# The last graph layer's weight products as seven block products, a block product accumulated in PSUM, and a plan with measured durations

## The chip, the cores and the metric

The kernel runs on one core of one Trainium2 chip. The metric is the device time of one execution in microseconds; the kernel before took 1390.6 us, the median of three executions between 1390.11 and 1391.59 us. The engines are named as in the profile: PE is TensorE (PEld its weight loads), DVE is VectorE, ACT is ScalarE, POOL is GpSimd, and SP is the queue that issues most transfers.

## The reference

Four graph layers act on 64 graphs of 256 nodes with 128 features, all in fp32, and each ends in a layer norm of the input plus the layer's output. Cut to what matters here:

```python
# layer 0: attention over pairs; layer 1: masked attention (both cut)
# layer 2: a gated update, five times
def step(h, _):
    m_in = jnp.einsum('nm,bmd->bnd', in_matrix, h)      # both matrices are adj
    m_out = jnp.einsum('nm,bmd->bnd', out_matrix, h)
    av = jnp.concatenate([m_in, m_out], axis=-1)
    u3 = h @ u3_w.T + u3_b
    z = sigmoid(av @ w3_w.T + w3_b + u3)
    r = sigmoid(av @ w4_w.T + w4_b + u3)
    hv = tanh(av @ w5_w.T + w5_b + (r * h @ u5_w.T + u5_b))
    return (1.0 - z) * h + z * hv, None
# layer 3: x, A x, A^2 x, A^3 x for two equal adjacencies, each with its weights
parts = [x[..., None], chebyshev(adj0, x, 3), chebyshev(adj1, x, 3)]
y = jnp.einsum('bnik,iok->bno', jnp.concatenate(parts, axis=3), weight_1)
x = layernorm(x + y)
```

Since both adjacencies are the same matrix A, layer 3 is x W0' + A x W1 + A^2 (x W2 + A x W3): W0' is the first weight plus the identity (the residual), and W1 to W3 are each the sum of two weights. The kernel takes it in this form.

## The kernel before

The 64 graphs are worked in 32 units of two. Ten units are in flight, one in each lane; a planner in the kernel's Python sorts all instructions by a greedy simulation with a duration and a latency for each, and then records them in that order. The planner's numbers decide the order on each engine, and nothing else.

A product of A (256 by 256, two by two blocks of 128) with a unit's features (two graphs, each two blocks of 128 columns) is done with seven block products in place of eight, with sums of blocks ahead (`block_sums`) and merges afterwards. `left_fast` does this 182 times, in layer 2 and at the start of layer 3:

```python
def left_fast(src, blk, mat, s, p1, m, by_pool):
    four = block_sums(src, blk, s, by_pool)        # three GpSimd instructions
    x, y = bank(), bank()                          # two PSUM banks
    ...
    one(x, 0, a(0), 0, 0, (src,))                  # one(): a product 128x128x128
    add(ACT, 280, lambda: nc.scalar.copy(p1.ap[:, 0:P], x.ap[:, 0:P]), (x,), (p1,))
    one(x, 1, a(1), 1, 0, (src,))
    one(y, 3, a(3), 3, 1, (src,), s.writers[-1:])
    one(y, 1, sm(0), 3, 0, (s,))
    one(y, 0, sm(1), 2, 0, (s,))
    one(x, 2, sm(2), 2, 1, (s,))
    one(y, 2, sm(3), 1, 1, (s,))
    merged(x, y, p1, m)                            # L872, L875, L877, L878

def merged(x, y, p1, m):
    # L872: m[0], m[3] = x[1:3] + p1                128x256 VectorE
    # L875: m[1:3] = y[0:2] + m[3]                  128x256
    # L877: m[3] = y[0] + m[2]                      128x128
    # L878: m[1:3] = y[2:4] + m[1:3]                128x256
```

In layer 3, `xT` and `aT` (x and A x, features on the partitions) are multiplied by the weights with eight products of 256 columns, whose results are a pair: the part for A^2 and the part that is added directly. The part for A^2 is copied by ScalarE, summed by VectorE and multiplied by A^2 (`a2f`) with seven block products that run into the same banks:

```python
for k, src in enumerate((xT, aT)):
    for (b, c), (ps, at) in home.items():          # four places in two banks
        add(PE, mm_ns(N), ... nc.tensor.matmul(
            gd(ps.ap)[:, at], bn(src.ap)[:, b, c * P : (c + 1) * P], w3.ap[:, k], ...))   # L1004
...
add(ACT, 370, lambda: nc.scalar.copy(sv[:, 0:4:3], gd(x.ap)[:, 0:3:2]), ...)              # L1009
add(ACT, 370, lambda: nc.scalar.copy(sv[:, 1:3], gd(y.ap)[:, 0:2]), ...)                  # L1010
block_sums(s, lambda g: sv[:, g], L["xT1"], -1 in BY_POOL)                                # on VectorE
... seven products (L1015), a ScalarE copy of the first (L1028)
merged(x, y, p1, out)
add(DVE, 240, ... out[3] += x[3] ...)                                                     # L1035
layernorm(u, L, y_pairs(out))
```

The last three units (`PLAIN = 3`) take another form, `layer3_end`: eight weight products and four products with A^2, all of 256 columns (L1048, L1055).

Of the kernel before, what the change touches and what calls it, by code (L numbers as in the profile page):

```python
# [32 lines left out]
PERIOD = 43e3  # L33
TAIL = 0.3
LATE = 6
PACE = 3.0
PACE_GATED = 1.56
# [4 lines left out]
HASTE = {"pe": 10e3, "act": 10e3, "dve": 10e3}  # L42
PLAIN = 3
# [26 lines left out]
class Plan:  # L70
# [5 lines left out]
    LATENCY = {"pe": 500, "dve": 400, "act": 400, "pool": 500, "sp": 4000}  # L76
# [127 lines left out]
def kernel(  # L204
# [58 lines left out]
    def lane_cells(k):  # L263
# [8 lines left out]
        for at, halves in (("e", (("r", "ex"), ("z",))), ("p", (("v",), ("xT1",)))):  # L272
            for half, names in enumerate(halves):
                over = [c[at]]
                for name in names:
                    c[name] = Cell(c[at].ap.rearrange("p g n -> p (g n)")[:, half * T : (half + 1) * T], over=over)
                    over = [*over, c[name]]
        c["x"] = cell(f"x_{k}", [P, UB, NC, D])
# [112 lines left out]
    add(ACT, 500, lambda: nc.scalar.copy(adjT.ap.rearrange("p c n -> p (c n)"), ps_adj.ap), (ps_adj,), (adjT,))  # L391
# [81 lines left out]
    add(ACT, 500, lambda: nc.scalar.copy(adjTp.ap.rearrange("p c n -> p (c n)"), ps_adjp.ap), (ps_adjp,), (adjTp,))  # L473
# [18 lines left out]
    w3 = cell("w3", [D, 2, 2, D])  # L492
    add(POOL, 480, lambda: nc.gpsimd.tensor_add(w3.ap[:, 0, 1, :], wk.ap[:, :, 0], ident.ap), (wk, ident), (w3,))
    for k in range(1, 4):
        add(POOL, 480, lambda k=k: nc.gpsimd.tensor_add(
            w3.ap[:, k % 2, 1 - k // 2, :], wk.ap[:, :, k], wk.ap[:, :, k + 3]), (wk,), (w3,))
# [10 lines left out]
    fast_blocks(a2f, a2T)  # L507
    plan.rank = None


    X = {}

# [17 lines left out]
    def feature_major(src, view, t):  # L530
        ps = bank()
        for g in range(G):
            add(PE, 110, lambda g=g: nc.tensor.transpose(ps.ap[:, g * P : (g + 1) * P], view(g), ident.ap),
                (src, ident), (ps,))
        add(ACT, 500, lambda: nc.scalar.copy(t.ap, ps.ap), (ps,), (t,))

    def turned(u, L, step):
# [8 lines left out]
        add(DVE, 1050, lambda: nc.vector.transpose(  # L546
# [33 lines left out]
    def layernorm(u, L, pairs, swap=False, centred=False):  # L580
# [11 lines left out]
        add(POOL, 1050, lambda: nc.gpsimd.tensor_tensor(rstd.ap, ve.ap, nhalf.ap, op=ALU.pow), (ve, nhalf), (rstd,))  # L592
        by_act = u >= TIGHT and plan.layer in NORM

        if by_act and not centred:
            mean = st.ap.rearrange("p k (j s) -> p k j s", j=2)[:, :, :, 1]
            if "shift" in SMALL:
                add(POOL, 280, lambda: nc.gpsimd.tensor_scalar_mul(
# [50 lines left out]
    def layer0(u, L):  # L649
# [47 lines left out]
        for b in range(UB):  # L697
            add(DVE, 520, lambda b=b: nc.vector.tensor_add(
                ev[:, b, :, 0:P].rearrange("p k (c i) -> p k c i", c=NC), rv()[:, b].rearrange("p c (i k) -> p k c i", k=2),
                neg0.ap[:, :, 0:P].rearrange("p k (c i) -> p k c i", c=NC)), (row, neg0), (e,), group=es)  # L700
# [8 lines left out]
        for b in range(UB):  # L709

            small(u, "s", 130, lambda eng, b=b: eng.tensor_scalar(
# [3 lines left out]
        for g in range(G):  # L715
            add(ACT, 400, lambda g=g: nc.scalar.activation(
# [4 lines left out]
        for g in range(G if SCALES and u >= TIGHT else 0):  # L721
            add(ACT, 320, lambda g=g: nc.scalar.activation(
# [33 lines left out]
    def layer1(u, L):  # L756
# [6 lines left out]
        for bs in [[b] for b in range(UB)] if u < HALVES else [list(range(UB))]:  # L763
# [3 lines left out]
            for b in bs:  # L767
                for g in range(b * NC, (b + 1) * NC):
                    add(ACT, 600, lambda g=g, b=b: nc.scalar.activation(  # L769
# [15 lines left out]
            for b in bs:  # L785
# [11 lines left out]
                for c in range(NC if SCALES and u >= TIGHT else 0):  # L797
                    add(ACT, 290, lambda b=b, c=c, ov=ov: nc.scalar.activation(
# [11 lines left out]
        add(ACT, 550, lambda: nc.scalar.activation(ex.ap, hp.ap, AF.Exp, bias=minus1.ap), (hp, minus1), (ex,))  # L810
        xf = X[u].ap.rearrange("p b c d -> p (b c d)")
        add(DVE, 600, lambda: nc.vector.scalar_tensor_tensor(hp.ap, ex.ap, 1.0, hp.ap, op0=ALU.min, op1=ALU.max), (ex, hp), (hp,))
        add(DVE, 600, lambda: nc.vector.tensor_add(hp.ap, hp.ap, xf), (hp, X[u]), (hp,))
# [11 lines left out]
    def block_sums(src, blk, s, by_pool):  # L825
# [5 lines left out]
        wide, narrow = (830, 480) if by_pool else (360, 220)  # L831
# [7 lines left out]
    def left_fast(src, blk, mat, s, p1, m, by_pool):  # L839
# [3 lines left out]
        def one(ps, at, lhs, k, c, cells, after=()):  # L843
            add(PE, mm_ns(P) + 4, lambda: nc.tensor.matmul(  # L844
                ps.ap[:, at * P : (at + 1) * P], lhs(), mat.ap[:, k, c * P : (c + 1) * P], start=True, stop=True,
                skip_group_check=True), (*cells, mat), (ps,), after, group=four)
# [8 lines left out]
        one(x, 0, a(0), 0, 0, (src,))  # L855
        add(ACT, 280, lambda: nc.scalar.copy(p1.ap[:, 0:P], x.ap[:, 0:P]), (x,), (p1,))  # L856
        one(x, 1, a(1), 1, 0, (src,))
        one(y, 3, a(3), 3, 1, (src,), s.writers[-1:])
# [4 lines left out]
        merged(x, y, p1, m)  # L863

    def merged(x, y, p1, m):
        mv = gd(m.ap)

        def pv(ps):
# [3 lines left out]
        add(DVE, 400, lambda: nc.vector.tensor_tensor(  # L872
            mv[:, 0:4:3], pv(x)[:, 1:3], p1.ap[:, 0:P].rearrange("p (o n) -> p o n", o=1).to_broadcast([P, 2, P]), op=ALU.add),
            (x, p1), (m,))
        add(DVE, 400, lambda: nc.vector.tensor_tensor(  # L875
            mv[:, 1:3], pv(y)[:, 0:2], mv[:, 3:4].to_broadcast([P, 2, P]), op=ALU.add), (y, m), (m,))
        add(DVE, 240, lambda: nc.vector.tensor_add(mv[:, 3:4], pv(y)[:, 0:1], mv[:, 2:3]), (y, m), (m,))  # L877
        add(DVE, 400, lambda: nc.vector.tensor_add(mv[:, 1:3], pv(y)[:, 2:4], mv[:, 1:3]), (y, m), (m,))  # L878

    def layer2(u, L):  # L880
        h, ht = turned(u, L, -1), X[u]
        for step in range(STEPS):
# [14 lines left out]
            if not fast:  # L897
                add(ACT, 500, lambda ps_m=ps_m: nc.scalar.copy(m.ap, ps_m.ap), (ps_m,), (m,))
# [15 lines left out]
            add(ACT, 600, lambda ps_g=ps_g, up=up: nc.scalar.activation(  # L914
                r.ap, ps_g.ap, AF.Tanh, bias=bias2.ap[:, 1:2], scale=0.5 / up), (ps_g, bias2), (r,))
            tanh_r = list(r.writers)
            add(DVE, 600, lambda h=h: nc.vector.scalar_tensor_tensor(r.ap, r.ap, 1.0, h.ap, op0=ALU.add, op1=ALU.mult),
# [4 lines left out]
            add(ACT, 600, lambda ps_g=ps_g, up=up: nc.scalar.activation(  # L922
# [6 lines left out]
            add(DVE, 600, lambda h=h, new=new: nc.vector.scalar_tensor_tensor(  # L929
                new.ap, z.ap, -1.0, h.ap, op0=ALU.add, op1=ALU.mult), (z, h), (new,))  # L930
            add(ACT, 600, lambda ps_v=ps_v, up=up: nc.scalar.activation(  # L931
                v.ap, ps_v.ap, AF.Tanh, bias=bias2.ap[:, 2:3], scale=1 / up), (ps_v, bias2), (v,))
            add(DVE, 600, lambda: nc.vector.scalar_tensor_tensor(v.ap, z.ap, 1.0, v.ap, op0=ALU.add, op1=ALU.mult),  # L933
                (v, z), (v,))
            add(DVE, 600, lambda new=new, part=part: nc.vector.scalar_tensor_tensor(
# [3 lines left out]
            if step < STEPS - 1 and far(u, step):  # L939
# [3 lines left out]
                add(DVE, 600, lambda h=h, v=v: nc.vector.transpose(  # L943
# [10 lines left out]
            if far(u, step):  # L954

                add(DVE, 600, lambda h=h, v=v: nc.vector.transpose(
# [13 lines left out]
            if step < STEPS - 1:  # L970
                add(ACT, 500, lambda ps_t=ps_t: nc.scalar.copy(L["ht"].ap, ps_t.ap), (ps_t,), (ht,))
# [11 lines left out]
    def layer3(u, L):  # L983
# [5 lines left out]
        else:  # L989
# [3 lines left out]
            add(ACT, 500, lambda: nc.scalar.copy(aT.ap, ps_a.ap), (ps_a,), (aT,))  # L993
# [6 lines left out]
        x, y = bank(), bank()  # L1000
        home = {(0, 0): (x, slice(0, 2)), (1, 1): (x, slice(2, 4)), (0, 1): (y, slice(0, 3, 2)), (1, 0): (y, slice(1, 4, 2))}
        for k, src in enumerate((xT, aT)):
            for (b, c), (ps, at) in home.items():
                add(PE, mm_ns(N), lambda k=k, src=src, c=c, b=b, ps=ps, at=at: nc.tensor.matmul(  # L1004
                    gd(ps.ap)[:, at], bn(src.ap)[:, b, c * P : (c + 1) * P], w3.ap[:, k],
                    start=(k == 0 and b == 0), stop=(k == 1), skip_group_check=True), (src, w3), (ps,), tail)
        four, sv = gd(L["xT1"].ap), gd(s.ap)
        copies = object()
        add(ACT, 370, lambda: nc.scalar.copy(sv[:, 0:4:3], gd(x.ap)[:, 0:3:2]), (x,), (s,), group=copies)  # L1009
        add(ACT, 370, lambda: nc.scalar.copy(sv[:, 1:3], gd(y.ap)[:, 0:2]), (y,), (s,), group=copies)  # L1010
        block_sums(s, lambda g: sv[:, g], L["xT1"], -1 in BY_POOL)
        t, p1, out = L["xT1"], L["v"], L["ht"]

        def one(ps, at, lhs, c, k, start, after=()):
            return add(PE, mm_ns(P) + 4, lambda: nc.tensor.matmul(  # L1015
                ps.ap[:, at * P : (at + 1) * P], a2f.ap[:, k // NC, k % NC * P : (k % NC + 1) * P], lhs(), start=start,
                stop=True, skip_group_check=True), (c, a2f), (ps,), after, group=four)

        def d(g):
            return lambda: sv[:, g]  # L1020

        def sm(k):
            return lambda: four[:, k]


        done = [one(x, 1, d(1), s, 2, False)]
        one(x, 0, d(0), s, 0, True, done)
        add(ACT, 280, lambda: nc.scalar.copy(p1.ap[:, 0:P], x.ap[:, 0:P]), (x,), (p1,))  # L1028
        done = [one(y, 3, d(3), s, 7, False), one(y, 2, sm(3), t, 3, False)]
        one(y, 1, sm(0), t, 6, True, done)  # L1030
        one(y, 0, sm(1), t, 4, True, done)
        one(x, 2, sm(2), t, 5, True, done)
        merged(x, y, p1, out)
        mv = gd(out.ap)
        add(DVE, 240, lambda: nc.vector.tensor_add(mv[:, 3:4], gd(x.ap)[:, 3:4], mv[:, 3:4]), (x, out), (out,))  # L1035
# [3 lines left out]
    def layer3_end(u, L, xT, aT, s, tail):  # L1039
# [11 lines left out]
        for c in range(NC):  # L1051
            add(ACT, 300, lambda c=c: nc.scalar.copy(s.ap[:, c * N : (c + 1) * N], ps[c].ap[:, 0:N]), (ps[c],), (s,), group=ps)
        for c in range(NC):
            for mc in range(NC):
                add(PE, mm_ns(N), lambda c=c, mc=mc: nc.tensor.matmul(  # L1055
                    ps[c].ap[:, N : 2 * N], a2T.ap[:, mc, c * P : (c + 1) * P], s.ap[:, mc * N : (mc + 1) * N],
                    start=False, stop=(mc == NC - 1), skip_group_check=True), (a2T, s), (ps[c],))
        pairs = [(ps[c], lambda c=c: view(c)[:, 1]) for c in range(NC)]
# [56 lines left out]
```

The softmax here doesn't subtract the row's maximum and nothing guards it: scores larger than these inputs give would overflow.

## Time and profile before

| | before |
|---|---|
| time, median of three | 1390.6 us |
| span of the profiled execution | 1390.3 us |
| mean granted TensorE clock | 1.000 |
| TensorE busy | 1379.5 us |
| VectorE busy | 1217.7 us |
| ScalarE busy | 909.1 us |
| GpSimd busy | 630.5 us |
| DMA moved | 147.12 MB |

A line of instruction groups reads: source line, engine, operation, output and inputs by the program's names, shapes, count; then the group's busy time in us and the mean of one in ns; then the idle time of the engine ahead of them and what ended it. Names of tiles that share memory may stand for one another (`e` holds the tiles `r` and `z`, `p` holds `v` and `xT1`). In a line of waits the three numbers are the sum in us, how often, and the longest. In the chain of work that ended last, a piece has its start, its length and its number of records.

### The profile page before, as it was taken

How to read it: one execution, taken by the hardware profiler on the slowest of the kernel's cores; microseconds unless marked ns; L12 is line 12 of the kernel's file. 1: busy time of each engine (PE TensorE's matmuls, PEld its weight loads, DVE VectorE, ACT ScalarE, POOL GpSimd, SP SyncE). 2: the span in 40 equal slices, each digit the busy share in tenths (PEclk: the TensorE clock that was granted, in tenths of full speed). 3: DMA queues.
4: the chain of work that ended last, by engine and by line, in shares of the span. 5: the costliest groups of instructions: out<-in, count | busy, mean ns of one | idle time of the engine just before them, and what ended most of it. 6: DMA issues, size and time to landing. Idle time of an engine off the chain costs nothing.

```text
span 1390.3 us, 23222 instructions
## 1 busy us (share of the span) xinstructions
PE 1379.5 (99%) x6891; PEld 967.8 (70%) x6891; DVE 1217.7 (88%) x2745; ACT 909.1 (65%) x2121; POOL 630.5 (45%) x1039
## 2 busy tenths in 40 slices
PE   9999999999999999999999999999999999999998
PEld 8776666677667777667767767776666666666777
DVE  6887999999888989989898999899889798988955
ACT  6988554655676676865776768877675556564544
POOL 4233344345354453544453554465444443644524
PEclk9999999999999999999999999999999999999999
DMA  4223454445454545554554544455544545544422
GB/s 119 49 60 95 98 113 98 116 109 121 107 121 106 118 105 114 122 118 112 112 117 105 124 111 113 105 111 125 118 106 98 114 108 104 123 100 107 104 64 61
DMA packets 530076, 147.12 MB, mean 106 GB/s; under 512 B 456480, under 2 KB 495136, under 8 KB 529952
## 3 DMA queue, kind: packets, MB, share of 16 engines
q1 hardware_dynamic: 529152, 145.13, 46.5%
q8 instruction: 55, 0.90, 0.3%
q14 instruction: 69, 0.57, 0.1%
q10 hardware_dynamic: 800, 0.52, 0.1%
HBM read 81.10 MB, written 64.46 MB: 105 GB/s over the span
## 4 chain that ended last, share of the span: by engine, by line
PE 94%; DVE 3%; ACT 1%; POOL 0%; issue 0%; DMA 0%; POOLq 0%; SPq 0%; DVEq 0%; ACTq 0%
PE ps L902 48%; PE ps L844 20%; PE ps L1004 7%; PE ps L780 4%; PE ps L743 4%; PE ps L1015 3%; PE ps L792 2%; PE ps L738 2%; PE ps L667 2%; PE ps L821 1%; PE ps L1048 1%; PE ps L1055 0%; DVE st L587 0%; PE ps L351 0%; PE ps L968 0%
## 5 line engine op out<-in xcount | busy, mean ns | idle before, releaser
L902 PE MATMUL ps<-m,gT 128*128 128x512 f32 x960 | 471.5, 593 | 0.9 <-DVE m L878 0.5
L902 PEld LDWEIGHTS ps<-m,gT 128*128 128x128 f32 x960 | 170.3, 190 | 136.8 <-issue 115.9
L589 POOL TENSOR_SCALAR ve<-st 128x4 f32<-128x4 f32 x110 | 34.9, 317 | 364.9 <-DVE st L587 347.1
L914 ACT ACTIVATE e<-ps,bias 128x512 f32<-128x512 f32 x160 | 109.7, 686 | 130.2 <-PE ps L902 125.8
L931 ACT ACTIVATE p<-ps,bias 128x512 f32<-128x512 f32 x160 | 110.0, 687 | 90.3 <-PE ps L902 87.7
L592 POOL TENSOR_TENSOR rstd<-ve,nhalf 128x4 f32<-128x4 f32 x126 | 145.6, 1156 | 43.8 <-DVE ve L589 33.7
L902 PE MATMUL ps<-e,u5T 128*128 128x512 f32 x320 | 163.4, 593 | 0.0
L922 ACT ACTIVATE e<-ps,bias 128x512 f32<-128x512 f32 x160 | 109.7, 686 | 80.7 <-PE ps L902 78.6
L844 PE MATMUL ps<-adjTp,e 128*128 128x128 f32 x968 | 148.2, 275 | 0.4 <-ACT e L856 0.4
L933 DVE SCALAR_TENSOR_TENSOR p<-e,p 128x512 f32<-128x512 f32 x160 | 117.2, 733 | 33.1 <-ACT p L931 32.1
L844 PEld LDWEIGHTS ps<-adjTp,e 128*128 128x128 f32 x968 | 131.0, 192 | 19.0 <-issue 14.5
L833 POOL TENSOR_TENSOR e<-ht 128x256 f32<-128x256 f32 x121 | 99.4, 821 | 89.0 <-DMA ht<-hb 67.9
L844 PEld LDWEIGHTS ps<-adjTp,ht 128*128 128x128 f32 x726 | 108.7, 191 | 40.8 <-issue 36.7
L844 PE MATMUL ps<-adjTp,ht 128*128 128x128 f32 x726 | 120.8, 275 | 0.0
L902 PEld LDWEIGHTS ps<-e,u5T 128*128 128x128 f32 x320 | 59.2, 190 | 65.9 <-issue 50.1
L611 ACT ACTIVATE x<-ht,ve,rstd 128x128 f32<-128x128 f32 x212 | 90.9, 487 | 13.9 <-POOL ve L600 13.6
L902 PE MATMUL ps<-xT,gT 128*128 128x512 f32 x192 | 98.3, 593 | 0.5 <-DVE m L872 0.5
L833 POOL TENSOR_TENSOR e<-x 128x256 f32<-128x256 f32 x61 | 48.2, 790 | 96.2 <-ACT x L611 83.9
L875 DVE TENSOR_TENSOR m<-ps,m 128x256 f32<-128x256 f32 x182 | 74.8, 413 | 13.4 <-PE ps L844 11.1
L769 ACT ACTIVATE e<-m,esd 128x256 f32<-128x256 f32 x116 | 84.5, 765 | 0.0
L872 DVE TENSOR_TENSOR m<-ps,e 128x256 f32<-128x256 f32 x182 | 74.4, 413 | 11.2 <-PE ps L844 6.9
L835 POOL TENSOR_TENSOR e<-e,ht 128x128 f32<-128x128 f32 x121 | 79.4, 657 | 5.9
(210 smaller groups left out, 3145.7 us busy)
## 6 DMA issues: line engine op xcount, KB each, us to landing
hb<-p SPq DMA_DIRECT2D x182, 256.0 KB, 2.1
ht<-hb SPq DMA_DIRECT2D x484, 64.0 KB, 2.5
xT<-hb SPq DMA_DIRECT2D x244, 64.0 KB, 2.5
m<-row SPq DMA_DIRECT2D x58, 256.0 KB, 3.6
hb<-p SPq DMA_DIRECT2D x124, 64.0 KB, 1.8
ht<-hb SPq DMA_DIRECT2D x31, 256.0 KB, 3.0
out_dram<-x SPq DMA_DIRECT2D x30, 256.0 KB, 2.4
m<-in_x_dram SPq DMA_DIRECT2D x88, 64.0 KB, 2.3
```

The costliest lines, as they stand in the source:

```text
L592: add(POOL, 1050, lambda: nc.gpsimd.tensor_tensor(rstd.ap, ve.ap, nhalf.ap, op=ALU.pow), (ve, nhalf), (rstd,))
L611: add(ACT, 400, lambda j=j, b=b, ch=ch, view=view, at=at, shift=shift, col=col: nc.scalar.activation(X[u].ap[:, b, ch, :], view()[:, j, :] ...
L769: add(ACT, 600, lambda g=g, b=b: nc.scalar.activation(e.ap[:, g, :].rearrange("p (c n) -> p c n", c=NC), ev()[:, b], AF.Prelu, bias=esd.ap ...
L833: add(by, wide, lambda: eng.tensor_sub(four[:, 0:2], blk(slice(2, 3)).to_broadcast([P, 2, D]), blk(slice(0, 4, 3))), (src,), (s,), group=ss)
L835: add(by, narrow, lambda: eng.tensor_sub(four[:, 2:3], four[:, 1:2], blk(slice(0, 1))), (src, s), (s,), group=ss)
L844: add(PE, mm_ns(P) + 4, lambda: nc.tensor.matmul(ps.ap[:, at * P : (at + 1) * P], lhs(), mat.ap[:, k, c * P : (c + 1) * P], start=True, st ...
L902: add(PE, mm_ns(T), lambda: nc.tensor.matmul(ps.ap, w(), rhs.ap, start=start, stop=stop, skip_group_check=True), (c, rhs), (ps,), after)
L914: add(ACT, 600, lambda ps_g=ps_g, up=up: nc.scalar.activation(r.ap, ps_g.ap, AF.Tanh, bias=bias2.ap[:, 1:2], scale=0.5 / up), (ps_g, bias2 ...
L922: add(ACT, 600, lambda ps_g=ps_g, up=up: nc.scalar.activation(z.ap, ps_g.ap, AF.Tanh, bias=bias2.ap[:, 0:1], scale=0.5 / up), (ps_g, bias2 ...
L931: add(ACT, 600, lambda ps_v=ps_v, up=up: nc.scalar.activation(v.ap, ps_v.ap, AF.Tanh, bias=bias2.ap[:, 2:3], scale=1 / up), (ps_v, bias2), ...
L933: add(DVE, 600, lambda: nc.vector.scalar_tensor_tensor(v.ap, z.ap, 1.0, v.ap, op0=ALU.add, op1=ALU.mult), (v, z), (v,))
L1004: add(PE, mm_ns(N), lambda k=k, src=src, c=c, b=b, ps=ps, at=at: nc.tensor.matmul(gd(ps.ap)[:, at], bn(src.ap)[:, b, c * P : (c + 1) * P], ...
```

## The change

It has three parts. First, the weight products of layer 3 use the scheme of seven block products too: the two by two blocks of weights (`w3f`, prepared once with their block sums) against the two "rows" x and A x, where each block product is 128 wide and done for two column blocks of nodes. GpSimd forms four sums of the inputs ahead of them, VectorE merges their results, and the block sums of the closing product with A^2 move from VectorE to GpSimd. 30 units do so (`PLAIN = 2`). Second, in `left_fast` the second block product is accumulated onto the first in PSUM, after ScalarE has copied the first out, instead of being added by VectorE. Third, the planner's durations are replaced by measured ones, and its settings of urgency and latency by others. The first part is meant to take work from TensorE, the second from VectorE, and the third to give an order that fits the chip.

```diff
-LATE = 6
-PACE = 3.0
-PACE_GATED = 1.56
+LATE = 5
+PACE = 3.5
+PACE_GATED = 1.5
-HASTE = {"pe": 10e3, "act": 10e3, "dve": 10e3}
-PLAIN = 3
+HASTE = {"pe": 20000.0, "act": 20000.0, "dve": 20000.0}
+PLAIN = 2
-    LATENCY = {"pe": 500, "dve": 400, "act": 400, "pool": 500, "sp": 4000}
+    LATENCY = {"pe": 600, "dve": 500, "act": 500, "pool": 500, "sp": 4000}
... (durations: ScalarE copies 500 -> 475, VectorE 600 -> 680, and so on)
 # left_fast
-        one(x, 0, a(0), 0, 0, (src,))
-        add(ACT, 280, lambda: nc.scalar.copy(p1.ap[:, 0:P], x.ap[:, 0:P]), (x,), (p1,))
-        one(x, 1, a(1), 1, 0, (src,))
+        one(x, 0, a(0), 0, 0, (src,), start=True)
+        held = [add(ACT, 160, lambda: nc.scalar.copy(p1.ap[:, 0:P], x.ap[:, 0:P]), (x,), (p1,))]
+        one(x, 0, a(1), 1, 0, (src,), held)
+        add(ACT, 160, lambda: nc.scalar.copy(gd(m.ap)[:, 0], x.ap[:, 0:P]), (x,), (m,), group=ms)
...
+        add(DVE, 200, lambda: nc.vector.tensor_add(gd(m.ap)[:, 3], gd(x.ap)[:, 2], p1.ap[:, 0:P]), (x, p1), (m,), group=ms)
-        add(DVE, 400, ... mv[:, 0:4:3], pv(x)[:, 1:3], p1 ...)
 # layer 3
-        ... eight products of 256 columns, two ScalarE copies, block_sums on VectorE
+        x, ya, yb, z = bank(), bank(), bank(), bank()
+        ... four GpSimd sums of 128x256 over x and A x
+        for c in range(NC):
+            one(x, 2 * c, blk(x0, c), (xT,), w3f, 0, start=not c, after=tail)
+        held = [add(ACT, 270, lambda: nc.scalar.copy(gd2(p1.ap), gd2(x.ap)[:, 0:3:2]), (x,), (p1,))]
+        for c in range(NC):
+            one(x, 2 * c, blk(a0, c), (aT,), w3f, 2, after=held)
+        for c in range(NC):
+            one(x, 2 * c + 1, blk(sums[2], c), (sb_,), w3f, 5)
+        ... and eight more: sums[1] by block 4 and sums[0] by block 6 into ya,
+        ... sums[3] by block 3 and a1 by block 7 into yb
+        ... VectorE: up = x[1::2] + p1 (256); mv = ya + up (512); up = ya[:256] + mv[256:] (256); mv = yb + mv (512)
+        ... GpSimd: block sums of the part for A^2 (256, 128, 128 columns)
+        ... seven block products with A^2 into z and x, one ScalarE copy
+        ... VectorE: five merges (256, 256, 128, 256, 256), the last adds the direct part
         layernorm(u, L, y_pairs(out))
```

## The prediction

> **What bounds the kernel now.** I read the page first (busy shares, then the chain that ended last), then TensorE's waits, then the chain in a late stretch, because the pieces there show what one product costs when nothing holds it up.
>
> ```profile
> span 1390.3 us, 23222 instructions
> PE 1379.5 (99%) x6891; PEld 967.8 (70%) x6891; DVE 1217.7 (88%) x2745; ACT 909.1 (65%) x2121; POOL 630.5 (45%) x1039
> ...
> PE 94%; DVE 3%; ACT 1%; POOL 0%; issue 0%; DMA 0%; POOLq 0%; SPq 0%; DVEq 0%; ACTq 0%
> ```
>
> TensorE is busy 99% of the span and the last chain is almost wholly its own. The waits of TensorE say how much of the rest could still be had:
>
> ```profile
> PE ps L351 <- POOL ident masks.py:199: 1.3, 1, 1.3
> PE ps L792 <- DVE m L872: 0.7, 1, 0.7
> PE ps L667 <- ACT xT L535: 0.6, 1, 0.6
> ...
> PE ps L902 <- ACT e L914: 0.2, 1, 0.2
> PE ps L792 <- ACT xT L783: 0.2, 1, 0.2
> ```
>
> There are nine lines, each a single wait, with 4.9 us in total. The busy sum by stretches shows TensorE's last work ending at about 1384.3; the 6.0 us after it are the last normalisation and store. So 1390.3 = 1379.5 + 4.9 + 6.0, within rounding: to shorten the kernel, TensorE must get less work. The prices, from the chain between 1344 and 1365 us (start, length, group, records):
>
> ```profile
> 1347.34 1.73 PE ps L1004 x8
> ...
> 1362.30 0.89 PE ps L1015 x8
> ```
>
> One fp32 product leaves two records in the trace (800 products 512 wide stand in the program, 1600 records in the trace). So a 128x256 product costs 1.73 / 4 = 0.432 us and a 128x128 product 0.89 / 4 = 0.2225 us. Two halves cost 0.445 us, 3% more than one whole.
>
> **What the skill says.** (1) The Trainium skill, "Perfetto Trace Analysis", Identifying the Most-Contended Engine: matmul busy time is a poor measure of nearness to the roofline, since matmuls are pipelined. So I checked it by spacing: summing, over all matmul records, the median distance from start to start for their width gives 1372.8 us, within 7 us of the busy time. Here the 99% is honest. (2) "TensorE: Matmul & The Clock Gate", Back-to-back issue gap: a matmul costs its columns plus a few ns. The trace agrees in form (median record spacing 112, 216 and 429 ns for 128, 256 and 512 columns); that is why splitting a product costs so little. (3) "SBUF — State Buffer", Who interferes with whom: a VectorE instruction with two SBUF inputs contends with a GpSimd instruction that reads SBUF; one with a PSUM input doesn't. The trace agrees: the four 128x512 scalar_tensor_tensor groups of layer 2 average 734 ns, but those with no GpSimd work beside them 680 ns; the adds at L872 average about 413 ns either way, because one input is PSUM.
>
> **The change part by part.**
>
> *Weight products of the last layer.* Before, 29 units of batch pairs do 8 products of 256 columns and 7 of 128 there, and three plain units do 12 of 256. After, 30 units do 14 + 7 products of 128, and two stay plain. The built programs agree: 427 more products 128 wide, 244 fewer 256 wide, everything else on TensorE the same. Per ordinary unit 8 x 0.432 - 14 x 0.2225 = 3.456 - 3.115 = 0.341 us saved, times 29 = 9.9 us. The unit that changes camp: 12 x 0.432 - 21 x 0.2225 = 5.184 - 4.673 = 0.5 us. Sum 10.4 us of TensorE work; with the program's counts and the median spacings above (244 x 0.432 - 427 x 0.224) it is 9.8. I take 10.1.
>
> *VectorE and GpSimd pay for it.* The rows I use:
>
> ```profile
> L872 DVE TENSOR_TENSOR m<-ps,e 128x256 f32<-128x256 f32 x182 | 74.4, 413 | 11.2 <-PE ps L844 6.9 <-ACT e L856 3.6
> L877 DVE TENSOR_TENSOR m<-ps,m 128x128 f32<-128x128 f32 x182 | 49.7, 279 | 0.6
> L833 POOL TENSOR_TENSOR e<-ht 128x256 f32<-128x256 f32 x121 | 99.4, 821 | 89.0 <-DMA ht<-hb 67.9 <-PE ps L902 10.0 <-PE ps L844 5.0
> L1009 ACT COPY e<-ps 128x256 f32<-128x256 f32 x29 | 10.8, 371 | 19.8 <-PE ps L1004 17.2 <-DVE m L878 2.6
> L856 ACT COPY e<-ps 128x128 f32<-128x128 f32 x182 | 47.9, 265 | 44.9 <-PE ps L844 41.5 <-DVE ht L812 1.9 <-DVE st L587 0.4
> ```
>
> In the last layer VectorE gets, per unit, two adds 128x512 (estimate 0.68 us each, from the 134 ns that 128 columns add between the rows of 256 and 128), six of 256 (0.413) and one of 128 (0.279): 4.1 us. It gives up the old merge (1.8 us) and the three block sums, which move to GpSimd (1.1 us). Over 30 and 29 units that is 124 - 84 = +40 us. GpSimd gets four sums of 128x256 (about 0.8 us each) and the three block sums (2.1 us): 5.3 us x 30 = +159 us, a busy share of about 57%. ScalarE loses one 0.37 us copy per unit, -10 us.
>
> *Left products of layers 2 and 3.* 182 of them. The second block product now adds onto the first in PSUM, once ScalarE has copied the first out; a second ScalarE copy takes the sum. VectorE's first merge shrinks from 256 to 128 columns: 182 x 0.134 = -24 us. ScalarE: 182 x 0.265 = +48 us. TensorE does the same products.
>
> *Sums.* VectorE 1218 + 40 - 24 = 1234, plus some 9 us of port contention (640 instructions, 54 ns lost on average now, growing with GpSimd's share from 45 to 57%): 1243, 90%. ScalarE 947, 69%. All stay under TensorE's 1369, and all lie beside it. On the path that sets the end only TensorE's 10.1 us count.
>
> *New waits on TensorE.* The held product: in the new order the TensorE work between the first block product and the one that accumulates on it is 0.67 us at least, over 1.30 in 95% of the 182. The round trip needs about 0.5 (0.2 until the copy starts, 0.265 for it, and the hand-over): it is covered unless ScalarE is over 0.8 us late. For the last layer's four adds and three GpSimd sums before the closing products, the distance is 5.1 us at least and 7.4 in the median; the chain's durations sum to 2 x 0.41 + 2 x 0.68 + 2.1 = 4.3 us. Covered too, with little room in a few units.
>
> *The plan.* Measured durations and new urgency settings only reorder; no work changes. They can touch the 4.9 us of waits, of which about 2 us belong to the first 40 us.
>
> **The rivals.** *A: TensorE work decides* (as above): 1390.6 - 10.1 = 1380.5. For it: one engine at 99%, nine small waits. *B: VectorE and GpSimd become the bound in the full stretches.* VectorE already works 184.65 of the 200 us between 200 and 400 us (92%), and GpSimd's extra reads lengthen its two-input instructions. Against: ten units are in flight, and at 90 to 92% TensorE lost 1.6 us in that stretch and nothing in the next ones. If each of the 30 units cost TensorE one added wait of 0.3 us, 9 us would be gone and the time would be 1389. *C: the new plan also removes the mid-run waits.* Those after 40 us are at most about 3 us: 1377.5. *D: the narrower products cost more than their columns*, since 14 weight loads replace 8 and the load must hide under a shorter product. Against: the 0.2225 us is taken from a run of 128-wide products that already load new weights each time. If each cost another 10 ns, 427 x 0.01 = 4.3 us would be lost: 1385. Four instead of two PSUM banks held in the last layer belong to B: a late bank makes TensorE wait in the same way.
>
> **Range and chances.** A is most likely; B and D pull up by a few us in part, C pulls down by one or two. I take 1380.3, with 1376.5 (A and all of C) to 1386 (half of the gain lost). 2% would be 27.8 us; TensorE's remaining work of 1362 us and the closing 6 us forbid a gain of that size, and a loss of it would need waits of 38 us: faster 0.01, same 0.97, slower 0.02.
>
> **What would show each step.** Right: TensorE's busy time near 1369 with its share still 99%, records +366 in all (2 x 183), GpSimd near 790, VectorE near 1243, ScalarE near 947, TensorE's waits still under 8 us. The held product should appear among TensorE's waits with under 2 us. Wrong: a TensorE share of 98% or less with waits on the last layer's GpSimd sums or adds (B), or 128-wide products spaced wider than 112 ns a record (D).

## The result and the profile after

The changed kernel takes 1398.45 us (median; 1397.92 to 1399.00), the kernel before 1391.09 us in the same comparison: a ratio of 1.0053, 95% interval 1.0036 to 1.0070. It is slower by about 7 us where 10 us less were predicted, outside the predicted range of 1376.5 to 1386.

The page of the changed kernel (span, busy sums, chain by engine), in the lines that answer those shown of before:

```profile
span 1396.1 us, 24423 instructions
PE 1376.1 (99%) x7257; PEld 971.6 (70%) x7257; DVE 1251.7 (90%) x2783; ACT 932.0 (67%) x2274; POOL 816.6 (58%) x1254
...
PE 78%; DVE 12%; POOL 4%; ACT 2%; issue 2%; DMA 1%; SPq 0%; POOLq 0%; DVEq 0%; ACTq 0%
```

TensorE is still "busy 99%", yet the last chain is TensorE's own only to 78% where it was 94%: VectorE and GpSimd now stand in it. TensorE's waits, the largest (sum in us, how often, longest):

```profile
PE ps L852 <- ACT e L864: 2.0, 1, 2.0
...
PE ps L1032 <- DVE e L1061: 1.1, 1, 1.1
PE ps L910 <- DVE m L886: 1.1, 3, 0.5
PE ps L1032 <- ACT e L1042: 0.9, 2, 0.5
...
```

All eleven lines sum to 8.8 us, against 4.9 before. That can't be all, so I made an account by spacing, from the one profiled execution of each kernel. Each matmul record is given the median distance to the next one for its width (112 ns for 128 columns, 216 for 256, 429 for 512); the sum of what the distances have beyond that is the wait. "Tail" runs from the start of the last matmul record to the end. About 1.3 us before the first matmul complete each row. All in us:

| kernel | span | products | waits to 40 us | waits 40 to 1340 us | waits after 1340 us | tail |
|---|---|---|---|---|---|---|
| before | 1390.3 | 1372.8 | 4.9 | 5.1 | 0.2 | 6.0 |
| changed | 1396.1 | 1363.2 | 4.5 | 16.3 | 0.2 | 10.6 |
| difference | +5.8 | -9.6 | -0.4 | +11.2 | 0.0 | +4.6 |

So the gain on TensorE is there (-9.6) and is spent twice: on mid-run waits (+11.2) and on a longer tail (+4.6). The busy share hides this, because a matmul's record (275 ns for 128 columns) reaches over the next ones, so a pause loses up to 160 ns from sight, and a product at half clock counts as busy.

**The tail.** The chain of the changed kernel from its last products on:

```profile
1384.72 1.13 PE ps L1032 x10
1385.85 0.03 issue
...
1385.95 0.44 DVE ht L1083
...
1388.65 0.68 DVE st L595 x2
...
1389.92 1.00 POOL rstd L600
...
1391.23 0.49 ACT x L619
...
1392.11 0.77 ACT x L619 x2
```

And before, after a last piece of TensorE that ends at 1384.33 us:

```profile
1384.42 0.44 DVE st L629
...
1385.14 0.70 POOL rstd L632
...
1387.14 0.46 ACT x L636
```

The unit that `PLAIN = 2` moved into the block form now ends last: five VectorE merges, shared with the neighbour's work, then the statistics of the whole unit, GpSimd's power, four ScalarE instructions and a store of 256 KB. Before, the last unit in the plain form needed no merge, normalised each half apart and stored by halves of 128 KB.

**The largest mid-run wait.** The pause at 373 us, followed back by the chain (start, length, what):

```profile
363.77 4.44 POOL rstd L600
368.21 1.83 POOL p L1025 x2
...
372.48 1.41 POOL rstd L600
...
375.27 0.17 ACT e L864
375.44 0.04 issue
375.48 0.71 PE ps L852 x4
```

ScalarE's copy for the held product (L864) is late because ScalarE waits behind a normalisation, whose GpSimd instructions stand behind one that took 4.44 us and behind the new sums (L1025). The same instruction over both kernels (min/median/max in ns), first before, then after:

```profile
L592 POOL TENSOR_TENSOR rstd<-ve,nhalf x126: 1003/1037/1657, 22.6 to 1381.9; 128x4 f32<-128x4 f32 x126
```

```profile
L600 POOL TENSOR_TENSOR rstd<-ve,nhalf x126: 1002/1038/4442, 23.1 to 1389.9; 128x4 f32<-128x4 f32 x126
```

What VectorE does meanwhile (timeline of the changed kernel, VectorE alone):

```profile
363.70 0.67 DVE L941 SCALAR_TENSOR_TENSOR p<-e,p 128x512 f32<-128x512 f32 x1
364.30 1.21 DVE L781 TENSOR_TENSOR p<-e,mask 128x1024 f32<-128x1024 f32 x1
365.43 0.68 DVE L943 SCALAR_TENSOR_TENSOR p<-p 128x512 f32<-128x512 f32 x1
366.03 0.68 DVE L937 SCALAR_TENSOR_TENSOR p<-e,p 128x512 f32<-128x512 f32 x1
366.63 0.68 DVE L925 SCALAR_TENSOR_TENSOR e<-e,p 128x512 f32<-128x512 f32 x1
367.24 0.70 DVE L662 STREAM_TRANSPOSE xT<-m 128x512 f32<-128x512 f32 x1
```

Five instructions with two SBUF inputs follow each other without a gap from 363.70 to 367.31 us. GpSimd's instruction, begun at 363.77, ends at 368.21, which is 0.97 us after VectorE's first one-input instruction starts, about its own undisturbed length of 1.04 us. The next GpSimd instruction starts at 368.19, so the engine was really held for so long. This is what the Trainium skill ("SBUF — State Buffer", Who interferes with whom) calls an exclusive lock on the shared port pair, and here a whole queue of VectorE instructions keeps it.

**Three theories.** Theory 1: GpSimd's additional work (+159 us planned, busy +186 measured; about 164 of them are the new instructions, the rest is older ones that take longer) collides with VectorE's two-input instructions on the port; delays run through chains until TensorE waits. 1a: by the port; 1b: because GpSimd is busier. Theory 2: the planner's new settings give an order with too little room. Theory 3: the new round trip TensorE, ScalarE, TensorE of the held product costs the time.

### The profile page after: what moved, and what is told of

It reads as the page before. It is cut to its first block, busy times and chain, and to the rows that moved or that the text cites. A ratio compares the mean times of both kernels' runs of the same rounds, so it can differ in the third digit from the quotient of the medians.

```text
span 1396.1 us, 24423 instructions
## 1 busy us (share of the span) xinstructions
PE 1376.1 (99%) x7257; PEld 971.6 (70%) x7257; DVE 1251.7 (90%) x2783; ACT 932.0 (67%) x2274; POOL 816.6 (58%) x1254
## 4 chain that ended last, share of the span: by engine, by line
PE 78%; DVE 12%; POOL 4%; ACT 2%; issue 2%; DMA 1%; SPq 0%; POOLq 0%; DVEq 0%; ACTq 0%
PE ps L910 40%; PE ps L852 16%; PE ps L1032 8%; PE ps L751 3%; PE ps L788 3%; PE ps L746 2%; POOL rstd L600 2%; PE ps L800 2%; PE ps L675 1%; PE ps L829 1%; DVE m L883 1%; DVE st L595 1%; DVE e L925 1%; DVE p L941 1%; DVE p L554 1%
## 5 line engine op out<-in xcount | busy, mean ns | idle before, releaser
L910 PEld LDWEIGHTS ps<-m,gT 128*128 128x128 f32 x960 | 165.7, 191 | 133.1 <-issue 102.5
L600 POOL TENSOR_TENSOR rstd<-ve,nhalf 128x4 f32<-128x4 f32 x126 | 156.0, 1239 | 38.9 <-DVE ve L597 26.6
L597 POOL TENSOR_SCALAR ve<-st 128x4 f32<-128x4 f32 x110 | 43.0, 391 | 224.3 <-DVE st L595 201.5
L841 POOL TENSOR_TENSOR e<-ht 128x256 f32<-128x256 f32 x121 | 106.5, 880 | 102.2 <-DMA ht<-hb 90.6
L852 PEld LDWEIGHTS ps<-adjTp,ht 128*128 128x128 f32 x726 | 119.1, 191 | 61.8 <-issue 50.7
L852 PEld LDWEIGHTS ps<-adjTp,e 128*128 128x128 f32 x968 | 131.2, 192 | 12.6 <-issue 9.5
L852 PE MATMUL ps<-adjTp,ht 128*128 128x128 f32 x726 | 135.9, 275 | 2.0 <-ACT e L864 2.0
L941 DVE SCALAR_TENSOR_TENSOR p<-e,p 128x512 f32<-128x512 f32 x160 | 121.5, 760 | 17.4 <-ACT p L939 16.8
L619 ACT ACTIVATE x<-ht,ve,rstd 128x128 f32<-128x128 f32 x216 | 94.6, 491 | 22.1 <-POOL ve L608 22.0
L867 ACT COPY m<-ps 128x128 f32<-128x128 f32 x182 | 47.5, 267 | 65.7 <-PE ps L852 55.9
L925 DVE SCALAR_TENSOR_TENSOR e<-e,xT 128x512 f32<-128x512 f32 x96 | 71.4, 746 | 8.6 <-ACT e L922 8.4
```

What stands on the lines that cost most here:

```text
L600: add(POOL, 1150, lambda: nc.gpsimd.tensor_tensor(rstd.ap, ve.ap, nhalf.ap, op=ALU.pow), (ve, nhalf), (rstd,))
L619: add(ACT, 400, lambda j=j, b=b, ch=ch, view=view, at=at, shift=shift, col=col: nc.scalar.activation(X[u].ap[:, b, ch, :], view()[:, j, :] ...
L841: add(by, wide, lambda: eng.tensor_sub(four[:, 0:2], blk(slice(2, 3)).to_broadcast([P, 2, D]), blk(slice(0, 4, 3))), (src,), (s,), group=ss)
L852: add(PE, mm_ns(P) + 4, lambda: nc.tensor.matmul(ps.ap[:, at * P : (at + 1) * P], lhs(), mat.ap[:, k, c * P : (c + 1) * P], start=start, s ...
L910: add(PE, mm_ns(T), lambda: nc.tensor.matmul(ps.ap, w(), rhs.ap, start=start, stop=stop, skip_group_check=True), (c, rhs), (ps,), after)
L925: add(DVE, 680, lambda h=h: nc.vector.scalar_tensor_tensor(r.ap, r.ap, 1.0, h.ap, op0=ALU.add, op1=ALU.mult), (r, h), (r,))
```

## The experiments

The strongest ones keep every instruction of the kernel in its place and change only what some instructions do; they leave part of the computation out, as said at each. The others are planned anew; where only the third last unit changes, the order stays the same up to about 1349 us. "Mid-run waits" are those from 40 to 1340 us in the account by spacing. Times are medians; the ratio to the kernel before in the same comparison has its 95% interval.

### GpSimd's four sums left out, same order

```diff
-            add(POOL, 800, lambda ...: nc.gpsimd.tensor_tensor(sums[k], i, j, op=op), ...)
+            add(POOL, 800, lambda: None, ...)
```

> The changed kernel with every instruction in its place and order, but the four GpSimd sums ahead of the last layer's weight products left out (120 instructions, about 105 us of GpSimd work; the products read what the tiles held before, so this leaves out part of the computation). Theory 1 (the added GpSimd work, which shares an SBUF port with VectorE's two-input instructions, delays chains until TensorE waits): the mid-run waits of 16 us fall to 5 to 8 us and the time falls by 8 to 11 us, to about 1388. Theory 2 (the new order and settings of the plan leave too little room): the order is the same, so the waits stay, and the time falls by under 3 us, to 1396 or more.

1388.36 us, ratio 0.9983 (0.9977 to 0.9990); mid-run waits 6.5 us in place of 16.3, tail 10.6 as in the changed kernel.

```profile
span 1386.5 us, 24229 instructions
PE 1369.7 (99%) x7257; PEld 969.2 (70%) x7257; DVE 1229.3 (89%) x2783; ACT 930.4 (67%) x2274; POOL 709.2 (51%) x1134
```

```profile
L600 POOL TENSOR_TENSOR rstd<-ve,nhalf x126: 1001/1037/4446, 22.2 to 1380.2; 128x4 f32<-128x4 f32 x126
```

GpSimd's 107 us are gone, VectorE's busy time falls by 22 us though it does the same work, and 10 us return. The GpSimd instruction of 4.44 us is still there (4446 ns, the longest in the line above), but TensorE's pause is gone: it took the blocked instruction and the sums behind it together. Theory 1 holds; theory 2 fails for this order, which has room enough without the sums.

### The sums replaced by memsets, same order

```diff
-            add(POOL, 800, lambda ...: nc.gpsimd.tensor_tensor(sums[k], i, j, op=op), ...)
+            add(POOL, 800, lambda k=k: [nc.gpsimd.memset(sums[k], 0.0) for _ in range(2)], ...)
```

> The changed kernel in the same order, with each of the four GpSimd sums of the last layer replaced by two memsets of the same 128x256 place (estimate: together about as long as one sum took, 0.7 us, from the 0.2 us of GpSimd's smallest rows; the products then read zeros, so part of the computation is left out). A memset reads nothing from SBUF. Theory 1a (GpSimd's sums hurt because their reads and VectorE's two-input instructions exclude each other on the shared port): the mid-run waits fall as without the sums, to 6 to 9 us, time about 1388 to 1390, and the 128x512 scalar_tensor_tensor mean falls by 10 ns or more. Theory 1b (they hurt because GpSimd is simply busier and its queue later): the waits stay at 12 us or more and the time at 1395 or more.

1391.21 us, ratio 1.0002 (0.9993 to 1.0010); mid-run waits 9.2 us. GpSimd is busy for 771.4 us, 62 us more than without the sums and 45 less than with them. The memsets take 0.31 us each. VectorE's 128x512 two-input instructions take 739 ns on average in place of 756. Leaving the sums out saves 9.8 us of mid-run waits; 7.1 of them are saved already when GpSimd does something shorter there that reads nothing. The time is 1.2 us over the window expected under theory 1a, and since the memsets are shorter than the sums, this run alone doesn't part port and load.

### VectorE's instructions with one input, same order

```diff
-    nc.vector.scalar_tensor_tensor(r.ap, r.ap, 1.0, h.ap, ...)      (and three like it)
+    nc.vector.transpose(r.ap, h.ap)
```

All GpSimd work stays, the sums too; the gating of layer 2 is left out. Each replaced instruction still writes the tile that it wrote, and so waits for the same tanh of ScalarE.

> The changed kernel in the same order with all GpSimd work, but the 640 two-input VectorE instructions of layer 2 (128x512, 0.68 us when alone) replaced by transposes of one input of the same shape (0.70 us), so that the gating is left out of the computation. Theory 1a (port): GpSimd's sum of durations falls by 60 us or more with no instruction of it over 2.5 us, the pause of TensorE at 373 us disappears, mid-run waits fall from 16 to 8 us or less, time 1388 to 1390. Theory 1b (GpSimd busier): waits and time stay within 3 us of the changed kernel.

1384.34 us, ratio 0.9947 (0.9932 to 0.9963): 14.1 us less than the changed kernel and nearly 4 us below the window expected under theory 1a. Mid-run waits 2.4 us.

```profile
PE 1367.6 (99%) x7257; PEld 970.1 (70%) x7257; DVE 1201.0 (87%) x2783; ACT 932.3 (67%) x2274; POOL 662.8 (48%) x1254
```

The same 1254 GpSimd instructions take 662.8 us in place of 816.6: 154 us of GpSimd's "work" was waiting for the port. The longest GpSimd instruction is now 2.05 us, and the pause at 373 us is gone. The replaced instructions take 0.69 us, longer than the originals alone, so VectorE has not been given lighter work; it too waits less. Theory 1a holds: with every sum in place, 13.9 of the 16.3 us of mid-run waits go with the collision. Theory 1b, the load alone, falls. The order, the settings, the PSUM banks and the held product are those of the changed kernel, so without the collision all of them together cost no more than the 2.4 us that remain. Since leaving out the sums also took 9.8 us away, the added reads and the two-input instructions do the harm together.

### The same edit in the kernel before, same order

> The kernel before in its own order, with the same 640 VectorE instructions of layer 2 replaced by one-input transposes (the gating is left out of the computation). If the port is what the change made worse: the kernel before has only 5 us of mid-run waits, of which 2 to 4 go, time 1387 to 1390, a gain much smaller than the 14 us that the same edit gave in the changed kernel. If the port cost both kernels alike: 1377 or so.

1388.65 us, ratio 0.9982 (0.9975 to 0.9990); mid-run waits 2.3 us in place of 5.1. GpSimd falls from 630.5 to 528.2 us:

```profile
PE 1377.7 (99%) x6891; PEld 967.3 (70%) x6891; DVE 1191.1 (86%) x2745; ACT 908.6 (66%) x2121; POOL 528.2 (38%) x1039
```

So the port costs the kernel before 2.4 us and the changed one 14.1. Both kernels have the same mid-run waits without it; what then stands between them, 1388.65 and 1384.34, is 4.3 us, close to the 9.6 us of products less the 4.6 us of the tail. This accounts for the change.

### The third last unit in its old form

```diff
-PLAIN = 2
+PLAIN = 3
```

> The changed kernel with the third last unit in the old closing form (PLAIN 3 in place of 2). Theory of the tail: the time from TensorE's last matmul to the end falls from 10.6 us to 6, TensorE's work grows by 0.5 us, the mid-run waits stay: 4 us less, about 1394.5. Rival (the tail is hidden or moves elsewhere, or the new order of everything changes more than the tail): a change under 2 us or in the other direction.

1395.54 us, ratio 1.0036 (1.0022 to 1.0050). The tail is 6.4 us, as expected; the start (+1.2) and the last stretch (+1.0) give part of it back. The order of the start is the same in both, so its 1.2 us show how much one execution can differ there. The tail is real; undoing it saved 3 us of the 4.6.

### The planner's settings apart from the rest

```diff
 the changed kernel with: LATE 5 -> 6, PACE 3.5 -> 3.0, PACE_GATED 1.5 -> 1.56, HASTE 20e3 -> 10e3, LATENCY 600/500/500 -> 500/400/400, PLAIN 2 -> 3
```

> The changed computation and durations, with the old planner settings (LATE, PACE, PACE_GATED, HASTE, LATENCY, PLAIN as in the kernel before). Theory 2 (settings): mid-run waits fall back to about 5 us and the tail to 6 us: about 1383. Theory 1 (GpSimd load): the tail falls to 6 us, the mid-run waits stay at 12 to 18 us: about 1394.

1419.23 us, ratio 1.0204 (1.0188 to 1.0219): mid-run waits 26.6 us, and 14.3 us of waits after 1340 us. And the reverse, the new settings in the kernel before:

> The kernel before with the new planner settings alone (LATE, PACE, PACE_GATED, HASTE, LATENCY; old durations, old products, PLAIN 3). Theory 2 (settings): mid-run waits grow from 5 to 12 us or more, time about 1398. Theory 1 (GpSimd load): within 3 us of the kernel before.

1396.66 us, ratio 1.0043 (1.0028 to 1.0058): mid-run waits 5.8 us as before, but 3.9 us of waits after 1340 us. Neither theory foresaw these sizes. The new settings aren't what slows the changed kernel; it needs them. Each set fits its own computation, at the end of the run above all. The new durations, the other half of the change's third part, were not tried apart from the rest.

### The accumulation alone, in the kernel before

```diff
-        one(x, 1, a(1), 1, 0, (src,))
+        one(x, 0, a(1), 1, 0, (src,), held)        (with its two ScalarE copies and the smaller merge)
```

> The kernel before with the accumulated second block product in the 182 left products alone (old settings, old last layer; durations new only in the lines touched). TensorE's work is the same, VectorE does 24 us less, ScalarE 48 us more. Theory 1: no GpSimd work is added, so within 4 us of the kernel before, with waits for the held product under 2 us. Theory 3 (the new round trip over ScalarE makes TensorE wait): waits of TensorE on the first copy of 5 us or more, time 1396 or more.

1394.30 us, ratio 1.0024 (1.0016 to 1.0032); mid-run waits 8.6 us, of which the view of waits puts 2.0 us on the two ScalarE copies. Theory 3 in its strong form (5 us on the first copy) fails; the 3.3 us lost are within what theory 1 allowed, and come with a new order.

### The accumulation undone in the changed kernel

> The changed kernel with PLAIN 3 and the accumulated second block product undone (VectorE adds it, as before; 182 ScalarE copies fewer, VectorE +24 us). Theory 3 (the round trip over ScalarE costs some 3 us, as the accumulation alone did in the kernel before): 2 to 4 us under the 1395.5 of PLAIN 3. Theory 1 (GpSimd and port decide, and VectorE's relief helps): equal or up to 4 us more.

1389.77 us, ratio 0.9992 (0.9983 to 1.0000), 5.8 us under its partner (the third last unit in its old form); mid-run waits 13.2 us. More than either theory said, but see the last run below, which turns the sign.

### Two other orders of the same instructions

```diff
-            add(DVE, 330, ... bn_stats ...)
+            add(DVE, 331, ... bn_stats ...)        (and 334)
```

> The changed kernel with PLAIN 3 and one planned duration 1 ns longer (331 in place of 330 for the layer norm's statistics): the same instructions in another order. If the order is a lottery: anywhere within 5 us of the 1395.5 of PLAIN 3, by the mid-run waits. If waits come from load alone: within 1.5 us of it.

> As draw1 with 334 in place of 330: another order. The spread of PLAIN 3, draw1 and draw2 is what an order by itself is worth; I expect 3 to 8 us between the lowest and the highest, all between 1389 and 1401, and GpSimd's busy time within 15 us in all three.

1393.70 us (ratio 1.0018, 1.0011 to 1.0025) and 1395.24 us (1.0025, 1.0013 to 1.0037); mid-run waits 12.6 and 15.5 us, GpSimd 801 and 792 us. GpSimd's spread, with 812 us in the first order, is 20 us and not under 15. A few nanoseconds in the plan put another instruction into two thirds or more of the places on each engine (with 331, 4808 of TensorE's 7239 records differ in line or tiles), and the three orders differ by 1.8 us, less than I expected. All three wait far more than the kernel before: high waits belong to the changed computation, not to one unlucky order.

### The layer norm's shift moved from GpSimd to VectorE

```diff
-SMALL = ("ve", "cu", "d", "elu", "shift")
+SMALL = ("ve", "cu", "d", "elu")        (with PLAIN = 3)
```

> The changed kernel with PLAIN 3, and the layer norm's shift done by one small VectorE instruction (about 0.15 us, 82 times, +12 us) in place of two GpSimd instructions (0.46 and 0.36 us on average now, 164 in all, -67 us). The order is planned anew. Theory 1 (GpSimd load and port): mid-run waits fall from 16 to about 10 us, time 1388 to 1391. Rival (any new order is a new draw and the load matters little): 1393 or more, no fall of the waits beyond 3 us.

1391.78 us, ratio 1.0010 (1.0001 to 1.0018), 1.9 to 3.8 us under the three orders above; mid-run waits 13.3 us. Between the two expectations: taking 56 us from GpSimd helps less than ending the collision did in the same order.

### One input kept in PSUM

Two of layer 2's four VectorE instructions read ScalarE's third tanh. Here ScalarE writes it back into its PSUM bank; nothing is left out:

```diff
-                v.ap, ps_v.ap, AF.Tanh, ...
+                ps_v.ap, ps_v.ap, AF.Tanh, ...
-            ... scalar_tensor_tensor(v.ap, z.ap, 1.0, v.ap, ...)    and    (new.ap, v.ap, part, new.ap, ...)
+            ... scalar_tensor_tensor(ps_v.ap, z.ap, 1.0, ps_v.ap, ...)    and    (new.ap, ps_v.ap, part, new.ap, ...)
```

> The changed kernel with PLAIN 3, computing everything, in which ScalarE writes the third tanh of each step of layer 2 back into its PSUM bank, so that two of the four VectorE instructions (320 of 640) have one input in PSUM and one in SBUF. The work of no engine changes; the bank is held some 2 us longer. The order is planned anew. Theory 1a (port): the mid-run waits fall from 16 us to about 8, GpSimd's busy time falls by 40 us or more, time about 1387. Theory 1b (GpSimd is merely too busy): no change, 1394 or more. Rival (banks): waits grow because a bank comes late, 1398 or more.

1390.97 us, ratio 0.9999 (0.9991 to 1.0008); the two instructions fall to 0.685 and 0.680 us on average (0.751 and 0.771 with the third last unit in its old form), GpSimd to 730.8 us, mid-run waits to 11.9 us. The port is relieved as expected, but the time falls by 4.6 us where 8.5 were expected. With the second tanh in PSUM too:

> As the one before, but the second tanh stays in its PSUM bank too and the product of both is written to PSUM, so that 480 of the 640 instructions read the port at most once. Theory 1a (port): mid-run waits 3 to 6 us, time about 1383. Rival (banks): two banks of each step are held some 2 us longer, TensorE waits for banks, 1392 or more.

1396.79 us, ratio 1.0038 (1.0023 to 1.0053). GpSimd falls further, to 695.3 us, but mid-run waits are 18.7 us. They now stand elsewhere: one pause of 3.2 us at 199 us, where the view of waits names VectorE's product in PSUM (3.4 us in two waits). The rival, held banks, is what this fits; I didn't separate it from a bad order. And in the kernel before:

> The kernel before with the third tanh kept in PSUM alone, planned anew. Theory 1a (port): the kernel before waits only 5 us in mid-run, so there is little to win: 1386 to 1391. Rival (banks): 1394 or more.

1400.35 us, ratio 1.0068 (1.0052 to 1.0085). Its mid-run waits are 4.6 us, so the banks show no harm there; 8.5 us of waits stand after 1340 us, most of them one wait of 5.8 us for a transfer. Why it comes late in this order stays open.

### Port relief and other parts together

> The changed kernel with PLAIN 3, the third tanh kept in PSUM (320 instructions freed of the port) and the accumulation undone: every instruction is needed, nothing is left out. Theory (port and round trip both cost): mid-run waits under 10 us, time 1384 to 1389, faster than the kernel before. Rival (orders are a lottery): 1389 to 1395.

1389.57 us, ratio 0.9991 (0.9984 to 0.9997), mid-run waits 11.8 us: the rival's window.

> The changed kernel with PLAIN 3, the third tanh kept in PSUM and the layer norm's shift on VectorE. If GpSimd's load still decides: mid-run waits fall from 12 to 8 us or less, time 1385 to 1388. If what is left is the order and VectorE at 90%: within 2 us of 1391, the time with the tanh in PSUM alone.

1378.66 us, ratio 0.9911 (0.9896 to 0.9925): faster than both kernels, by 12 and by 20 us, with nothing left out. Its page and all of TensorE's waits:

```profile
span 1377.2 us, 24251 instructions
PE 1368.1 (99%) x7239; PEld 969.8 (70%) x7239; DVE 1233.6 (90%) x2856; ACT 933.8 (68%) x2274; POOL 685.0 (50%) x1083
```

```profile
PE ps L788 <- DVE p L781: 1.7, 1, 1.7
PE ps L353 <- POOL ident masks.py:199: 1.3, 1, 1.3
PE ps L1032 <- POOL m L1067: 0.3, 1, 0.3
```

Its account: products 1363.6, start 4.9, mid-run waits 1.2, tail 6.0 us. This is near the time that the prediction expected of the change. Neither expectation foresaw so low a time. VectorE is at 90% here as well, so that load alone doesn't force the waits. It is one order only; how much of the gain belongs to the port and how much to this order isn't shown, and the next run warns of the second.

> As the one before with the accumulation undone. If the round trip over ScalarE costs 1.5 to 5 us as in the pairs before: that much less than its partner, 1383 to 1388. If VectorE at 91% is the next bound: equal or slower than its partner.

1393.89 us, ratio 1.0020 (1.0013 to 1.0027): 15 us more than its partner. Mid-run waits 17.4 us, of which 5.6 lie in three pauses between 948 and 956 us, with GpSimd at only 681.2 us. In the three pairs, undoing the accumulation changed the time by -5.8, -1.4 and +15.2 us. The expectation of a gain failed. So whether the accumulation helps is not settled by these runs; it depends on the order it comes with.

## Why the prediction was wrong

*TensorE's work:* right. Predicted 10.1 us less, measured 9.6; records +366, exactly as counted; the 128-wide spacing stays at 112 ns, so rival D had no part.

*"The 6.0 us after it are the last normalisation and store"* was taken as a constant, and I counted the third last unit only by its products (0.5 us saved). It became the last to end: the tail grew by 4.6 us. This is a term that was missing, and it could have been seen: the block form ends in five merges that the plain form lacks.

*"Here the 99% is honest"* misread the sum. With 1372.8 us of products, 17.5 us of the span are left: 6.0 of tail, 1.3 before the first matmul, and 10.2 of waits, twice the 4.9 that the view of waits names. 1379.5 + 4.9 + 6.0 came out right because the busy time held the rest. So rival C's "at most about 3 us" after the first 40 us were 5.3.

*"All stay under TensorE's 1369, and all lie beside it"* is the step that failed. Rival B was named and even sized (30 units x 0.3 us, 1389), then set aside because VectorE at 90 to 92% had cost TensorE little. The load was nearly as predicted (VectorE 1251.7 for 1243, ScalarE 932.0 for 947, GpSimd 816.6 for 790). But I treated the port as a small surcharge on VectorE: 9 us. VectorE's 128x512 two-input instructions rose from 733 to 756 ns on average over 672 of them, 16 us. The larger side was GpSimd's, which I gave no term at all. If each GpSimd instruction's length above the shortest 5% of its kind is counted as blocked, it was blocked for 140 us before and 197 us after, once for 3.4 us on end. That lateness goes into normalisations and block sums, for which later products wait. Added waits on TensorE came to 11.2 us, near the 9 that rival B had been given. With the collision taken away in the same order, mid-run waits were 2.4 us and nothing but the tail stood against the gain. Which engine's lateness, GpSimd's or VectorE's, reached TensorE more often the runs don't separate.

*"Covered unless ScalarE is over 0.8 us late":* the held products show 2.3 us of waits (2.0 on the first copy and 0.3 on the second), near the 2 us I allowed; the 2.0 are the one pause above, which comes from GpSimd.

*"They can touch the 4.9 us of waits"* was too narrow a view of the plan. With the changed computation the new settings saved 24 us (1395.54 against 1419.23); with the old one they cost 5.8 us.

*What would show it right:* I named a busy time near 1369 us, a share of 99% and waits under 8 us as signs. The share stayed at 99% while TensorE waited 21 us in all (4.5 + 16.3 + 0.2): it is no sign. The view of waits gave 8.8 us, only just over. The busy time did warn: 1376.1 us with less work, since waits hide in it. The spacing sum that I used for the kernel before was the right view, and I should have named it as the test.

## What to carry to other kernels

Work moved from a full engine to GpSimd is not free merely because GpSimd is half idle. Here its reads of SBUF and VectorE's two-input instructions kept each other waiting: 154 of its 816.6 us went when 640 of those had one input. What counts is both together, and one input in PSUM took an instruction out of the contest (0.75 to 0.77 us became 0.68). Judge a matmul-bound kernel by the spacing of its matmuls and by the tail after the last one, not by TensorE's busy share. Where a scheduler orders everything, test a cause with the order kept and only the content changed; here three orders of the same instructions differed by 2 us, and once a new order came with 15 us for a change that was expected to be worth 5 at most.

## What the runs showed of the hardware

A GpSimd instruction of 1.04 us took 4.44 us behind five back-to-back two-input VectorE instructions: VectorE did not hand over the port between them. The two next longest of the same GpSimd instruction (2.58 us each, at 55.78 and 253.94 us) stand behind two and three of them, and end 0.96 and 0.94 us after VectorE's first instruction that doesn't have two SBUF inputs.

A pause of TensorE of 2.05 us at 373 us was followed by a spell of half clock, from 376.17 to 379.59 us (busy times of TensorE, its weight loads, VectorE, ScalarE and GpSimd in three stretches; the granted clock is the third column from the end):

```profile
372.00:376.00 4.00, 1.95 (x17) 1.76 (x17) 3.25 (x6) 2.79 (x10) 3.92 (x7) 1.00 0.19 70
376.00:380.00 4.00, 4.00 (x18) 3.52 (x17) 3.72 (x9) 3.13 (x8) 3.92 (x8) 0.57 0.51 113
380.00:384.00 4.00, 4.00 (x37) 3.95 (x35) 3.98 (x8) 2.71 (x6) 3.64 (x6) 1.00 0.69 169
```

TensorE is "busy" for all of the second row with 18 matmul records where the next four us hold 37. The spell costs about 1.7 us (half of 3.4), nearly as much again as the pause. The Trainium skill ("TensorE: Matmul & The Clock Gate", HAM oscillation) warns of idle gaps above about 3.4 us; here one of 2.05 us was followed by half clock, and so was the same pause with the third last unit in its old form, while a pause of 3.2 us in the kernel with both tanhs in PSUM was followed by none. What decides isn't shown.
